# Issuing four read-back transfers from ScalarE's queue, and copying the null scores later on GpSimd

## The chip, the cores and the metric

The kernel runs on one core of one Trainium2 chip. The core has five instruction streams that run side by side and meet only at semaphores: TensorE (PE, with its weight loads shown as PEld), VectorE (DVE), ScalarE (ACT), GpSimd (POOL) and SyncE (SP). In this kernel SP does nothing but issue DMA transfers. Each stream executes in the order in which the program wrote it: an instruction that waits holds everything behind it on its own engine. The metric is device time in microseconds (us).

## The reference

64 sequences of 128 tokens and 512 features go through one attention layer with a residual:

```python
xn  = layernorm(x, g_in)
q   = (xn @ Wq).reshape(64, 128, 16, 64) * 64**-0.5     # 16 heads
k, v = split(xn @ Wkv)                                  # one head of keys and values for all
k   = concat([null_k, k]); v = concat([null_v, v])      # one null key ahead of the 128
sim = q @ k.T + concat([null_bias, attn_bias])          # (64, 16, 128, 129)
sim = where(causal or masked_key, -big, sim)            # the null key is never masked
out = softmax(sim) @ v                                  # (64, 128, 16*64)
x   = x + layernorm(out @ Wo, g_out)
```

Everything is float32.

## The kernel before, in words

**Steps and groups.** The work is a software pipeline written out by hand in `step(n)`, one step for each sequence n. Sequences are normalised and projected in groups of four, so a period is four steps, some 69 us. In one step the kernel is at several places at once: the softmax of sequence n+1, the scores of n+2, the values of n, the query projection of the group that holds n+6, and the tokens of n+11. The order of all instructions is the order of the text (`manual_schedule`); nothing is moved afterwards.

**Two matrix products in seven parts.** The query projection and the output projection are each computed as seven products of half-size blocks. Sums of blocks of the tokens (`token_sum`, xS, L403, on POOL) feed products 4 to 7. A product may be accumulated on top of an earlier one in the same PSUM tile, after the earlier one has been copied out: ACT's `keep` (L432) and `out_keep` (kyp, L725), or DVE's copy kyu (L723). So PE's seventh output product (pyX, L711) cannot start before DVE has made kyu.

**Scores.** S[b] (tile `s`, 128 partitions x 8 rows x 194 columns, two buffers) holds the scores of a sequence. POOL first writes bias plus mask into it (`bias_add`, L458, 3.45 us), then copies 16 null scores for each partition into its first and last column (`null_copy`, L467, from tile nv). DVE adds the products and takes maxima (L511, L516), ACT takes exponentials row by row (L525: eight rows of 65 for the lower half, eight of 129 for the upper), DVE inverts the sums (`rinv`, L542) and POOL scales (`scale`, L546).

**Transfers that turn things round.** The scaled weights are transposed in 32 x 32 blocks by DVE (sb, L572), and 14 transfers (`blocks_move`, L592) put the blocks in place (aTb) for PE's values (po, L641). The tokens go the same way through memory, once a group: DVE transposes 32 x 32 blocks (xb, L277), `tokens_out` (L286) writes 1 MB to a scratch tensor xd, and one step later `tokens_in` (L294) reads it back as four transfers of 256 KB into xT. `nulls_move` has ACT copy (L331, L332) and SP transfer (L333, L336) the null scores into nv.

**SP's order around the change.** In the step before: the 1 MB xd, then 14 block transfers, two stores, the residual, a sequence. In the step of the change: the four xT, two nv, and later the next 14 blocks. All of these were issued by SP.

**Semaphores of transfers.** The framework gives the transfers eight completion semaphores, handed out in the order of the program, with one transfer outstanding on each. The instruction that issues a transfer first waits until the transfer that last had its semaphore has landed, whichever engine issued that one.

Of the kernel before, what the change touches and what calls it, by code (L numbers as in the profile page):

```python
# [17 lines left out]
def kernel(  # L18
# [58 lines left out]
    nc = tc.nc  # L77
# [212 lines left out]
    def tokens_in(g):  # L290
        xT[g] = gp.tile([P, GB, KC, N], FP, tag="xT", name=f"xT_{g}")
        xd = xds.pop(g).rearrange("(i p) j e -> j p i e", p=Q)
        for j in range(NQ):
            nc.sync.dma_start(  # L294
                out=xT[g][j * Q : (j + 1) * Q].rearrange("p i c n -> p i (c n)"),
                in_=xd[j],
            )
# [27 lines left out]
    def nulls_move(g, ts):  # L325

        if ts.start == 0:
            nv[g] = hp.tile([P, GB, DH + H], FP, tag="nv", name=f"nv_{g}")
        lo, hi = slice(0, DH), slice(DH, P)
        n1, n0 = slice(DH, DH + R8), slice(DH + R8, DH + H)  # L330
        nc.scalar.copy(nv[g][lo, ts, n1], vs[g][lo, ts, n0])  # L331
        nc.scalar.copy(nv[g][hi, ts, n0], vs[g][hi, ts, n1])  # L332
        nc.sync.dma_start(  # L333
            out=nv[g][hi, ts, 0 : DH + R8], in_=vs[g][lo, ts, 0 : DH + R8]
        )
        nc.sync.dma_start(out=nv[g][lo, ts, n0], in_=vs[g][hi, ts, n0])  # L336
# [118 lines left out]
    def bias_add(b):  # L455
        g, t = divmod(b, GB)
        S[b] = sp.tile([P, R8, ROW], FP, tag="s", name=f"s_{b}")
        nc.gpsimd.tensor_tensor(  # L458
            S[b][:, :, 1 : ROW - 1],
            biasp,  # L460
            mneg[g][:, t].unsqueeze(1).broadcast_to([P, R8, NL + N]),
            ALU.add,
        )

    def null_copy(b):
        g, t = divmod(b, GB)
        nc.gpsimd.tensor_copy(  # L467
            S[b][:, :, 0 : ROW : ROW - 1],
            nv[g][:, t, DH:].rearrange("p (k e) -> p e k", k=2),
        )  # L470
# [215 lines left out]
    def out_sums(p):  # L686

        yS[p] = bp.tile([P, HC, N], FP, tag="yS", name=f"yS_{p}", bufs=1)
        h11, h12 = oT[p][:, lo_c], oT[p][:, hi_c]
        h21, h22 = oT[p + 1][:, lo_c], oT[p + 1][:, hi_c]  # L690
        nc.gpsimd.tensor_tensor(yS[p], h21, h22, ALU.add)
        nc.gpsimd.tensor_tensor(h21, h11, h21, ALU.subtract)
        nc.gpsimd.tensor_tensor(h11, yS[p], h11, ALU.subtract)  # L693
        nc.gpsimd.tensor_tensor(h12, h12, h11, ALU.subtract)

    def out_product(p, k, pool, tag, start=True):
        key = "y" + tag
        if start:
            prod[key] = pool.tile([P, HE], FP, tag=tag, name=f"py{tag}_{p}_{k}")
        a, b = oT[p], oT[p + 1] if p + 1 in oT else None  # L700
        h, w = {
            1: lambda: (a[:, lo_c], e11),
            2: lambda: (a[:, hi_c], e21),
            3: lambda: (a[:, hi_c], e22),
            4: lambda: (b[:, hi_c], wT[:, 3]),
            5: lambda: (yS[p], wT[:, 0]),
            6: lambda: (a[:, lo_c], wT[:, 1]),
            7: lambda: (b[:, lo_c], wT[:, 2]),
        }[k]()
        for c in range(HC):  # L710
            nc.tensor.matmul(  # L711
                prod[key],
                h[:, c, :],
                w[:, c, :],
                start=(start and c == 0),
                stop=(c == HC - 1),
                skip_group_check=not start,
            )
# [113 lines left out]
    def step(n):  # L832
        def ok(b, end=B):
            return 0 <= b < end
# [16 lines left out]
        if second:  # L851
            out_sums(p5673)
        elif ok(n + 2) and n >= 0:
            bias_add(n + 2)
            null_copy(n + 2)
        if third:
            pair_pow(p4)
        for m in mns:
# [37 lines left out]
        if (n + 7) % GB == 0 and 2 <= (n + 7) // GB < NG:  # L896
            tokens_in((n + 7) // GB)
# [8 lines left out]
                token_sum(qg, k)  # L906
        if second and ok(n + 2):
            bias_add(n + 2)
            null_copy(n + 2)
        if ok(n + 1) and fill:  # L910
            exps_half(n + 1, 0)
        if part == 3 and ok(n + 3):
            nulls_move((n + 3) // GB, slice(0, GB - 1))
        if part == 0 and ok(n + 2):
            nulls_move((n + 2) // GB, slice(GB - 1, GB))
        if first:
            out_product(p12, 1, ps_y, "X")
        if fast and n % 2 == 0:
# [157 lines left out]
    for n in range(-6, B - 1):  # L1076
        step(n)
        if n == -6:
            for kc in range(2):
                weights_kv(kc)  # L1080
            for kc in range(2, KC):
                weights_kv_prod(kc)
            load_late()
        if n == -5:
            for kc in range(2, KC):
                weights_kv(kc)
            causal(0)
            mask_neg(0)
            weight_sums()
# [48 lines left out]
```

## Time and profile before

| | |
|---|---|
| median of 3 runs | 1194.3 us (1191.9 to 1194.69) |
| profiled execution, its own time | 1188.5 us |
| its span | 1186.7 us |
| PE busy | 1117.3 us, 94% of the span |
| ACT busy | 684.9 us, 58% |
| POOL busy | 745.0 us, 63% |
| DVE busy | 793.4 us, 67% |
| granted TensorE clock, mean | 0.988 |
| DMA | 129.91 MB, mean 109 GB/s |

A line of a timeline reads: start, duration, engine, source line, operation, output<-inputs, shape, count, and in brackets the idle time of the engine before it and what ended that. In the tables of waits: engine, line, what it waited for, us in total, times, longest. "SPq" is SP's queue.

### The profile page before, as it was taken

The page shows a single profiled execution, that of the slowest core. Times are in us where ns is not written, and L with a number is a line of the kernel's source. Part 1 is how long each engine was busy: PE and PEld are TensorE (multiplying, and loading weights), DVE is VectorE, ACT ScalarE, POOL GpSimd, SP SyncE. Part 2 cuts the span into 40 slices and gives each one's busy share as a digit, 9 for nine tenths or more (in the row PEclk, how much of TensorE's full clock was granted, in tenths as well). Part 3 has the DMA queues.
Part 4 walks back from the last instruction along what each step waited for, and adds up shares of the span by engine and source line. Part 5 has one row for each costly group of instructions (what it writes and reads, how often), then busy time and mean ns, then how long its engine had stood idle before and what let it go on. Part 6 is the DMA issues. An engine that isn't in the chain of part 4 may idle for free.

```text
span 1186.7 us, 24481 instructions
## 1 busy us (share of the span) xinstructions
PE 1117.3 (94%) x8284; PEld 877.3 (74%) x8284; DVE 793.4 (67%) x1680; ACT 684.9 (58%) x2712; POOL 745.0 (63%) x588
## 2 busy tenths in 40 slices
PE   6877999999999999999999999999999999999786
PEld 4454787887878787887878788787878878887443
DVE  6554577676767867776776677677767756766442
ACT  3344665655666566565755656566565656655451
POOL 5454876567675756667665665767566576656432
PEclk9998999999999999999999999999999999999889
DMA  6313335343543535353353535344453533322221
GB/s 183 119 35 108 95 98 125 120 120 97 144 112 105 131 123 120 97 158 96 108 119 122 129 89 155 99 127 105 126 123 103 140 86 119 83 75 77 84 78 45
DMA packets 107852, 129.91 MB, mean 109 GB/s; under 512 B 29264, under 2 KB 72528, under 8 KB 105936
## 3 DMA queue, kind: packets, MB, share of 16 engines
q1 hardware_dynamic: 106912, 127.29, 39.2%
q8 instruction: 67, 1.10, 0.4%
q10 hardware_dynamic: 816, 1.05, 0.2%
q14 instruction: 57, 0.47, 0.1%
HBM read 54.86 MB, written 31.46 MB: 73 GB/s over the span
## 4 chain that ended last, share of the span: by engine, by line
PE 61%; SPq 12%; DMA 12%; DVE 7%; ACT 4%; POOL 2%; issue 2%; DVEq 0%; ACTq 0%; POOLq 0%
PE pa L421 13%; PE pyX L711 11%; SPq L592 10%; PE po L641 6%; PE pyY L711 6%; PE pc L421 5%; DMA xT<-xd 5%; PE ps L487 4%; PE pk L307 4%; PE py L661 3%; PE pw L421 3%; PE pyw L711 2%; DMA aTb<-sb 2%; ACT s L525 2%; PE ps L498 2%
## 5 line engine op out<-in xcount | busy, mean ns | idle before, releaser
L525 ACT ACTIVATE s<-s,nmax 128x65 f32<-128x65 f32 (+1 forms) x1024 | 372.3, 368 | 7.3 <-DVE nmax L516 6.9
L458 POOL TENSOR_TENSOR s<-biasp,mneg 128x1536 f32<-128x1536 f32 x64 | 220.9, 3451 | 127.8 <-DVE sb L572 124.9
L546 POOL TENSOR_TENSOR s<-s,rinv 128x512 f32<-128x512 f32 (+1 forms) x128 | 188.9, 1477 | 113.2 <-DVE nmro L753 81.5
L525 ACT ACTIVATION_READ_ACCUMULATOR s<-s,nmax 128x1 f32 x1024 | 194.6, 190 | 0.0
L649 ACT ACTIVATE oT<-po,nv 128x512 f32<-128x512 f32 x128 | 81.0, 680 | 166.2 <-PE po L641 166.1
L711 PE MATMUL pyX<-wT,oT 128*128 128x256 f32 x696 | 164.7, 379 | 1.2 <-POOL oT L693 0.7
L432 ACT COPY ku<-pa 128x256 f32<-128x256 f32 x120 | 44.7, 372 | 178.0 <-PE pa L421 176.4
L711 PEld LDWEIGHTS pyX<-wT,oT 128*128 128x128 f32 x696 | 131.9, 190 | 20.1 <-POOL oT L693 1.1
L511 DVE TENSOR_TENSOR s<-ps,s 128x512 f32<-128x512 f32 (+1 forms) x128 | 121.6, 950 | 26.4 <-PE ps L498 15.0
L421 PE MATMUL pa<-xS,wq 128*128 128x256 f32 x480 | 123.6, 380 | 2.4 <-ACT ku L432 1.4
L516 DVE TENSOR_REDUCE nmax<-s 128x8 f32<-128x520 f32 (+1 forms) x128 | 120.4, 940 | 6.0 <-POOL s L467 3.7
L641 PE MATMUL po<-aTb,vs 128*64 128x256 f32 (+1 forms) x768 | 109.7, 397 | 3.5 <-DMA aTb<-sb 1.8
L572 DVE STREAM_TRANSPOSE sb<-s 128x1536 f32<-128x1536 f32 x62 | 109.6, 1769 | 2.2 <-DMA xT<-xd 1.3
L421 PEld LDWEIGHTS pa<-xS,wq 128*128 128x128 f32 x480 | 86.8, 190 | 13.0 <-ACT ku L432 2.4
L487 PEld LDWEIGHTS ps<-kT,qT 64*128 64x128 f32 x1024 | 65.5, 196 | 31.6 <-issue 20.7
L487 PE MATMUL ps<-kT,qT 64*128 64x128 f32 x1024 | 78.1, 294 | 5.4 <-DVE s L511 5.4
L442 DVE TENSOR_TENSOR qT<-pw,kp 128x256 f32<-128x256 f32 x60 | 25.4, 423 | 77.2 <-ACT kp L432 77.2
L641 PEld LDWEIGHTS po<-aTb,vs 128*64 128x64 f32 (+1 forms) x768 | 44.9, 138 | 39.5 <-issue 27.3
L421 PE MATMUL pc<-xS,wS 128*128 128x256 f32 x240 | 63.3, 386 | 7.8 <-POOL xS L403 6.9
L245 POOL TENSOR_TENSOR rstd<-rstd,nhalf 128x1 f32<-128x1 f32 x64 | 35.8, 559 | 54.7 <-DVE rstd L244 54.7
L307 PE MATMUL pk<-wkv,xT 128*128 128x144 f32 x488 | 69.9, 286 | 0.0
L421 PE MATMUL pa<-xS,wS 128*128 128x256 f32 x240 | 67.8, 405 | 0.0
(122 smaller groups left out, 2162.5 us busy)
## 6 DMA issues: line engine op xcount, KB each, us to landing
aTb<-sb SPq DMA_DIRECT2D x372, 64.0 KB
x<-in_x_dram SPq DMA_DIRECT2D x64, 256.0 KB
res<-in_x_dram SPq DMA_DIRECT2D x64, 256.0 KB
out_dram<-y SPq DMA_DIRECT2D x64, 256.0 KB
aTb<-sb SPq DMA_DIRECT2D x496, 32.0 KB
xd<-xb SPq DMA_DIRECT2D x14, 1024.0 KB
xT<-xd SPq DMA_DIRECT2D x56, 256.0 KB
wo<-in_L_cond_Wo_dram SPq DMA_DIRECT2D x1, 2048.0 KB
```

What stands on the lines that cost most here:

```text
L307: nc.tensor.matmul(pkv, xT[g][:, t, kc, :], wkv[:, kc, :], start=(kc == 0), stop=(kc == KC - 1),)
L421: nc.tensor.matmul(prod[tag], w[:, kc, f * P : (f + 1) * P], t[:, :, kc, :], start=(start and kc == 0), stop=(kc == HK - 1), skip_group_ch ...
L458: nc.gpsimd.tensor_tensor(S[b][:, :, 1 : ROW - 1], biasp, mneg[g][:, t].unsqueeze(1).broadcast_to([P, R8, NL + N]), ALU.add,)
L487: nc.tensor.matmul(pv[:, r, f, :], qT[g][rows, f, t, 1].rearrange("p u i -> p (u i)"), kT[b][rows, :], start=True, stop=True,)
L511: nc.vector.tensor_tensor(sv, pss.pop((b, hf)), sv, ALU.add)
L516: nc.vector.tensor_reduce(nmax[b][:, hf], S[b][:, :, WITH_NULL[hf]], AX.X, ALU.max, negate=True)
L525: nc.scalar.activation(row, row, AF.Exp, bias=nmax[b][:, hf, k : k + 1], accum_out=rsum[b][:, hf, k : k + 1],)
L546: nc.gpsimd.tensor_tensor(sv, sv, rinvs.pop((b, hf)).unsqueeze(2).broadcast_to([P, R8, sv.shape[2]]), ALU.mult,)
L572: nc.vector.transpose(sb.rearrange("p j e q -> p e j q"), S[b][:, :, 1 : ROW - 1].rearrange("p e (j k) -> p e j k", k=Q),)
L592: nc.sync.dma_start(out=aT_of(b)[dst, is_].rearrange("p s e q -> p s (e q)"), in_=sb[src, js].rearrange("p s e q -> p s (e q)"),)
L641: nc.tensor.matmul(po[u][r * DH : (r + 1) * DH, half], vals, aT_of(b)[rows, slots, r * NF : (r + 1) * NF], start=True, stop=True,)
L711: nc.tensor.matmul(prod[key], h[:, c, :], w[:, c, :], start=(start and c == 0), stop=(c == HC - 1), skip_group_check=not start,)
```

## The change

Two edits. `tokens_in` issues its four transfers from ACT's queue in place of SP's, at the same place of the text; on ACT this is between two runs of four lower exponentials of sequence n+1. And `null_copy(n + 2)` is written later in the step, behind POOL's lower scaling, the first two token sums and the calls of `nulls_move`. No operation is added or left out.

```diff
@@ tokens_in
         for j in range(NQ):
-            nc.sync.dma_start(
+            nc.scalar.dma_start(
                 out=xT[g][j * Q : (j + 1) * Q].rearrange("p i c n -> p i (c n)"),
                 in_=xd[j],
             )
@@ step
         elif ok(n + 2) and n >= 0:
             bias_add(n + 2)
-            null_copy(n + 2)
...
         if second and ok(n + 2):
             bias_add(n + 2)
-            null_copy(n + 2)
         if ok(n + 1) and fill:
             exps_half(n + 1, 0)
         if part == 3 and ok(n + 3):
             nulls_move((n + 3) // GB, slice(0, GB - 1))
         if part == 0 and ok(n + 2):
             nulls_move((n + 2) // GB, slice(GB - 1, GB))
+        if ok(n + 2) and n >= 0:
+            null_copy(n + 2)
```

In the built program of the changed kernel, the four issues on ACT have these waits, in every group from the second read-back on: the first for xd and for the first of the 14 block transfers of the step before; the second for the seventh of them; the third for the eleventh; the fourth for the fourteenth. In the first read-back the last of the block transfers is waited for by the fourth issue too.

## The prediction

> **What bounds the kernel now.** I read the page's busy line first, then the chain that ended last, then the waits of PE, POOL and SP, and at last one group of four steps on the timeline.
>
> ```profile
> PE 1117.3 (94%) x8284; PEld 877.3 (74%) x8284; DVE 793.4 (67%) x1680; ACT 684.9 (58%) x2712; POOL 745.0 (63%) x588
> PE 61%; SPq 12%; DMA 12%; DVE 7%; ACT 4%; POOL 2%; issue 2%; DVEq 0%; ACTq 0%; POOLq 0%
> ```
>
> PE bounds it. From 150 to 1030 us, the steady part, PE is busy for 863.9 of 880 us. So about 16 us there, some 18 for all 14 groups that read tokens back, are the most that shorter waits can give; a delay that PE sees costs its full length.
>
> ```profile
> PE po L641 <- DMA aTb<-sb: 18.3, 11, 5.1
> PE pc L421 <- POOL xS L403: 6.9, 9, 1.9
> POOL s L467 <- DMA nv<-vs: 51.5, 12, 5.4
> SPq L592 <- DMA xT<-xd: 22.9, 42, 1.3
> ```
>
> These are what the change aims at. SP's block issues (L592) end waits on the read-back 42 times, three in each of 14 groups. That is the semaphore rule at work: an issue is held until the landing of the transfer that last used its semaphore. In the group at 523 us the four xT, by the trace's landing events, land at 531.3, 532.3, 533.7 and 534.5, and SP issues its 3rd to 6th block at 531.28, 532.34, 533.72 and 534.48. So the blocks are late, and with them PE's po; POOL's null copy waits for nv, queued behind the same read-back, and holds the token sums that PE's pc needs.
>
> **The change, first part: the read-back on ACT.** Taken away from SP: four issues, 1.9 us in a group, in front of two nv transfers and 14 blocks. Put on ACT, after the qT copy:
>
> ```profile
> 515.52 0.37 ACT L439 COPY qT<-pa 128x256 f32<-128x256 f32 x1
> 515.79 0.35 ACT L525 ACTIVATE s<-s,nmax 128x65 f32<-128x65 f32 x1
> ...
> 518.35 0.35 ACT L725 COPY kyp<-pyY 128x256 f32<-128x256 f32 x1
> ...
> 519.38 0.36 ACT L432 COPY kp<-pa 128x256 f32<-128x256 f32 x1
> ...
> 526.78 1.27 ACT L649 ACTIVATE oT<-po,nv 128x512 f32<-128x512 f32 x2 [4.33 <-PE po L641]
> ```
>
> ACT reaches the place at 515.8. But the fourth issue waits for the fourteenth block of the step before, and SP is then in the middle of issuing those:
>
> ```profile
> 512.04 9.04 SPq L592 DMA_DIRECT2D aTb<-sb  x14
> 521.13 1.08 SPq L791 DMA_DIRECT2D out_dram<-y  x2
> 522.25 0.45 SPq L125 DMA_DIRECT2D res<-in_x_dram  x1
> 522.75 0.60 SPq L119 DMA_DIRECT2D x<-in_x_dram  x1
> 523.45 1.88 SPq L294 DMA_DIRECT2D xT<-xd  x4
> ```
>
> By the landing events the first block lands at 514.1, the 7th at 517.8, the 11th at 520.4 and the 14th at 522.6; xd landed at 513.8. So the first issue passes at once, and the fourth is held until 522.6. Over the 13 groups that follow the first, that landing is 6.7 to 7.6 us, in the mean 7.0, behind ACT's arrival. One issue takes 0.43 to 0.5 us with 0.1 around it, so ACT resumes 7.0 + 0.6 = 7.6 us late.
>
> Behind it on ACT stand twelve exponentials, two null copies, kyp and kp. DVE waits for kp, and PE for DVE:
>
> ```profile
> 519.77 0.42 DVE L442 TENSOR_TENSOR qT<-pw,kp 128x256 f32<-128x256 f32 x1 [1.91 <-ACT kp L432]
> 520.82 0.42 DVE L723 COPY kyu<-pyX 128x256 f32<-128x256 f32 x1 [0.62 <-PE pyX L711]
> 521.48 1.89 PE L711 MATMUL pyX<-wT,oT 128*128 128x256 f32 x8
> ```
>
> DVE makes qT as soon as kp is there, then kyu, and PE's seventh output product starts 0.24 us after kyu. The one reserve on this path is the 0.62 us that DVE waited for PE. So PE stands still for 7.6 - 0.6 = 7.0 us in each group. The exponentials end, the upper scaling runs and sb is made as much later, so nothing catches up; ACT's 4.33 us of idle time ahead of oT comes too late on this path.
>
> Two costs are added for which no row stands. Blocks and read-back now share the DMA engines. Between 516 and 520 us the engines are 0.27 busy, so I take 0.4 us more for the 14th landing; nothing at one end, 2 us at the other (the 2.0 us that one transfer's issue to landing takes, once more). And an idle PE loses its clock:
>
> ```profile
> 562.70 0.38 PE L641 MATMUL po<-aTb,vs 64*64 64x256 f32 x2
> 563.02 1.08 PE L641 MATMUL po<-aTb,vs 128*64 128x256 f32 x8
> 564.04 1.16 PE L487 MATMUL ps<-kT,qT 64*128 64x128 f32 x16
> ...
> 1143.01 1.12 PE L641 MATMUL po<-aTb,nv 64*64 64x256 f32 x4 [4.53 <-DVE y L773]
> 1144.05 1.97 PE L641 MATMUL po<-aTb,vs 128*64 128x256 f32 x8
> 1145.96 2.08 PE L487 MATMUL ps<-kT,qT 64*128 64x128 f32 x16
> ```
>
> After 4.53 us of idle time the same work, 0.65, 1.08 and 1.16 us when the clock is up (0.65 is the same row at 1122 us), takes 0.5 + 0.9 + 0.9 = 2.3 us more; after 5.14 us (at 93 us) 1.8 and after 3.61 (at 1127) 2.0. Two gaps of 2.3 and 2.65 us cost nothing. At 7 us I take 2.0, between 0 and 2.3.
>
> The sum: 13 x (7.0 + 0.4 + 2.0) = 122 us. In the first group (ACT arrives at 109.7, the 14th block lands at 115.5) PE already waits 2.65 us for blocks, so I take 4 there, 2 to 7.
>
> What it gives: xT lands some 7 us earlier and the next 14 blocks start after it, so SP's waits and PE's po waits go (6.4 us of them in the steady part, and 2 for the clock lost at 543). The store, which takes over a semaphore from the first xT, finds it landed.
>
> On splitting queues the Trainium skill (DMA: Bandwidth & Descriptors, Issuing engines are not separate DMA queues) says that transfers from all engines run on the same 16 DMA engines and that a second issuing engine saves only the time to issue. That speaks against a gain beyond SP's 1.9 us a group, 27 us at most; the rows put the gain elsewhere, in landings that hold SP's issues, and the loss in a wait on ACT that the rule doesn't mention. By the rule alone the sum would lie between 1162 and 1189 us on the profiled execution.
>
> **Second part: the null copy.** It moves on POOL past two small powers, the lower scaling and, once a group, two token sums; no transfer and no other queue is passed. The copy takes 0.2 us. Its reader is DVE's lower maximum, some 10 us later in the step, so lateness up to 5 us is covered. The sums no longer stand behind a wait for nv: PE's pc waits go, 4.1 us in the steady part. In steps with no wait nothing changes.
>
> Gains together: at least 4 us (pc alone), at most 18 to 20 (all of PE's idle time and the clock loss). I take 13, the two named waits with the clock loss.
>
> Sum: 1188.5 + 122 + 4 - 13 = 1301 us for the profiled execution. That execution was 5.8 us below the median, so 1307 us against 1194.3.
>
> **The rivals.**
> 1. *Only the issues cost.* The blocks would have to land before ACT's arrival. Then ACT loses 4 x 0.5 = 2.0 us, PE 1.4, in 14 groups 20 us, against 13 of gain: 1201. For it: the first three issues do find their landings within 4.6 us, while ACT has slack later. Against it: the fourteenth block is issued at 520.5, 4.7 us after ACT's arrival.
> 2. *The change pays.* If ACT's delay stays under DVE's 0.62 us, PE loses nothing and the waits go: 1194 - 18 = 1176. It decides where the delay falls below about 1.5 us a group (0.6 of reserve, 0.9 of gain). For it: 51.5 and 22.9 us of waits on POOL and SP do go. Against it: four issues alone take 2.0 us.
> 3. *The stall is smaller than I count.* PE keeps its clock, or the engines use the pause to work off what made PE wait elsewhere: 1188.5 + 13 x 7.0 + 2 - 20 + 5.8 = 1267 at the least.
> 4. *It spreads.* Contention takes its 2 us in all groups: 1188.5 + 13 x 11.3 + 7 - 4 + 5.8 = 1344.
>
> **How the numbers follow.** My forecast, 1285 to 1330, has 0.60; rival 3 (1250 to 1285) 0.17; rival 4 0.11; rival 1 0.06; rival 2 0.06. The range that leaves out no more than 0.2 goes from 1255 to 1335. A measurement of this kernel can tell 0.3%, 3.6 us, from no change. Slower gets the forecast, 3, 4 and half of rival 1: 0.91; faster rival 2: 0.06; the same 0.03.
>
> **What the profile after would show.** Right: in each group ACT idle for about 7 us ahead of L525 with a block transfer as releaser; DVE's qT waiting for kp about as long; PE idle for about 7 us ahead of pyX with kyu (L723) as releaser, 14 times, 90 to 105 us together; matmuls after it at nearly double time and the mean clock below 0.988; SP's waits on xT, POOL's on nv and PE's on xS near nothing. Wrong: if ACT's idle time is about 2 us a group, the issues aren't held and rival 1 holds; if ACT is held and PE isn't, there is a reserve that I missed; if PE stalls and its clock stays, the sum is some 26 us too high.

## The result, and the profile after

The changed kernel takes 1323.0 us (median of 4 runs, 1320.8 to 1323.93), the kernel before in the same comparison 1194.5 us. The ratio is 1.1098, with a 95% interval from 1.1053 to 1.1144: 11% slower. The profiled execution took 1322.9 us, its span is 1320.8 us, and the mean granted clock is 0.937 (0.988 before).

The page of the changed kernel: its span, the busy line, the granted clock by slices, the shares of the chain that ended last, and the costliest group of instructions (after the bars: busy us and mean ns of one, then the idle time ahead of it with what ended that).

```profile
span 1320.8 us, 24479 instructions
PE 1144.6 (87%) x8284; PEld 897.9 (68%) x8284; DVE 789.9 (60%) x1680; ACT 686.0 (52%) x2712; POOL 744.4 (56%) x588
PEclk9988989989899898989989898998989989899979
PE 67%; SPq 10%; DMA 7%; ACT 7%; DVE 5%; issue 2%; POOL 1%; ACTq 0%; DVEq 0%; POOLq 0%
...
L711 PE MATMUL pyX<-wT,oT 128*128 128x256 f32 x696 | 189.3, 420 | 121.1 <-DVE kyu L723 120.4
```

Every engine does the work it did before, with the same count of instructions. PE is busy 27.3 us longer for the same 8284 matmuls: the clock, which stands at 8 tenths or less in 16 of the 40 slices (3 before). The queue of ACT, where the transfers now are, has 0% of the chain; so the share of a queue does not show this loss.

The waits of PE, ACT and DVE in the changed kernel (what for, us in total, times, longest):

```profile
PE pyX L711 <- DVE kyu L723: 120.4, 14, 10.0
PE po L641 <- DMA aTb<-sb: 9.5, 4, 5.1
...
PE po L641 <- DMA nv<-vs: 7.1, 1, 7.1
...
ACT s L525 <- DMA out_dram<-y: 124.1, 12, 11.0
...
DVE rinv L542 <- ACT s L525: 164.9, 64, 10.6
DVE qT L442 <- ACT kp L432: 82.6, 57, 2.8
```

The growth of the span, 134.1 us, is made of three parts. PE waits 120.4 us for kyu ahead of pyX, where before it waited 0.5. Thirteen of the fourteen gaps are new; they measure 7.67 to 10.03 us, in the mean 9.22, and make 119.9 us. PE's busy time gives 27.3 us, of which 24.6 lie in the group that follows the gap (189.3 against 164.7 us). The rest, 13.1 us less, is net of the first group, where PE now waits 7.1 us (by the line for nv) and waited 2.65 for a block: PE's other waits are 17.5 us shorter. The group in the kernel before:

```profile
L711 PE MATMUL pyX<-wT,oT 128*128 128x256 f32 x696 | 164.7, 379 | 1.2 <-POOL oT L693 0.7
```

One group of the changed kernel on the timelines of SP, ACT, DVE and PE (start, duration, and in brackets the idle time before and what ended it; "ACTq" is ACT's queue):

```profile
570.08 9.05 SPq L592 DMA_DIRECT2D aTb<-sb  x14
```

```profile
573.51 0.37 ACT L439 COPY qT<-pa 128x256 f32<-128x256 f32 x1
573.57 10.46 ACTq L294 DMA_DIRECT2D xT<-xd  x4
584.08 0.35 ACT L525 ACTIVATE s<-s,nmax 128x65 f32<-128x65 f32 x1 [10.20 <-DMA out_dram<-y]
```

```profile
585.55 0.20 DVE L542 RECIPROCAL rinv<-rsum 128x8 f32<-128x8 f32 x1 [9.74 <-ACT s L525]
...
588.06 0.42 DVE L442 TENSOR_TENSOR qT<-pw,kp 128x256 f32<-128x256 f32 x1 [2.31 <-ACT kp L432]
588.40 0.42 DVE L723 COPY kyu<-pyX 128x256 f32<-128x256 f32 x1
```

```profile
576.92 1.89 PE L711 MATMUL pyX<-wT,oT 128*128 128x256 f32 x8
578.65 1.03 PE L421 MATMUL pc<-xS,wS 128*128 128x256 f32 x4
588.88 3.78 PE L711 MATMUL pyX<-wT,oT 128*128 128x256 f32 x8 [9.20 <-DVE kyu L723]
592.45 2.34 PE L711 MATMUL pyY<-wo,oT 128*128 128x256 f32 x8
```

Read from top to bottom: SP is still issuing its 14 block transfers when ACT reaches the read-back at 573.57. ACT's four issues take until 584.03 and then the exponentials go on. DVE stands at rinv, then at qT, then makes kyu; PE starts 9.20 us late, and its first eight matmuls take 3.78 us in place of 1.89, the next eight 2.34: 2.3 us for the clock.

What ended ACT's wait is the point at which the line misleads. It names the store, because a store's event was the last seen just then. In the program the fourth issue of this group waits for the fourteenth block of the step before; the trace has that block landing at 583.70 and the fourth issue at 583.73. SP had issued this block at 578.51, so it was 5.19 us on its way. In the group at 523 us of the kernel before, it was issued at 520.47 and landed at 522.55: 2.08 us. In the mean of the 13 later groups it is 5.0 us against 2.1. The 3.1 us between them are in no row of the kernel before.

The text ahead of the prediction is wrong for two of the 14 read-backs. In the first, the fourth issue waits for the eleventh block, the third for the first transfer of the read-back itself, and none for the fourteenth block. In the last, the fourth issue (at 1131.82) waits for the read-back's own second transfer (landed at 1131.80), and the fourteenth block lands only at 1133.57; ACT is idle for 8.7 us there and PE for 7.67. In the other 12 the fourth issue follows the landing of the fourteenth block.

### The profile page after: what moved, and what is told of

It reads as the page before. It is cut to its first block, busy times and chain, and to the rows that moved or that the text cites. A ratio compares the mean times of both kernels' runs of the same rounds, so it can differ in the third digit from the quotient of the medians.

```text
span 1320.8 us, 24479 instructions
## 1 busy us (share of the span) xinstructions
PE 1144.6 (87%) x8284; PEld 897.9 (68%) x8284; DVE 789.9 (60%) x1680; ACT 686.0 (52%) x2712; POOL 744.4 (56%) x588
## 3 DMA queue, kind: packets, MB, share of 16 engines
q8 instruction: 66, 1.08, 0.4%
## 4 chain that ended last, share of the span: by engine, by line
PE 67%; SPq 10%; DMA 7%; ACT 7%; DVE 5%; issue 2%; POOL 1%; ACTq 0%; DVEq 0%; POOLq 0%
PE pyX L711 15%; PE pa L421 13%; SPq L592 10%; PE pyY L711 6%; PE po L641 6%; PE pc L421 5%; ACT s L525 5%; PE ps L487 4%; DMA aTb<-sb 4%; PE pk L307 3%; PE pyw L711 3%; PE pw L421 3%; PE py L661 3%; PE ps L498 2%; DVE sb L572 2%
## 5 line engine op out<-in xcount | busy, mean ns | idle before, releaser
L711 PE MATMUL pyX<-wT,oT 128*128 128x256 f32 x696 | 189.3, 420 | 121.1 <-DVE kyu L723 120.4
L711 PEld LDWEIGHTS pyX<-wT,oT 128*128 128x128 f32 x696 | 144.8, 211 | 149.7 <-DVE kyu L723 126.0
L542 DVE RECIPROCAL rinv<-rsum 128x8 f32<-128x8 f32 x128 | 24.0, 189 | 165.0 <-ACT s L525 164.9
```

What stands on the lines that cost most here:

```text
L711: nc.tensor.matmul(prod[key], h[:, c, :], w[:, c, :], start=(start and c == 0), stop=(c == HC - 1), skip_group_check=not start,)
```

## The experiments

All of them compute the whole reference. Where one run of a kernel stands, it is its profiled execution; the kernel before had medians of 1192.1 to 1196.5 us beside them.

**1. Each edit alone.** Before, with only the queue changed:

```diff
-            nc.sync.dma_start(
+            nc.scalar.dma_start(
```

> Only the first edit: the four read-back issues on ACT, the null copy at its old place. Theory (ACT held by the semaphores of the block transfers): the whole loss is here, PE's idle time ahead of pyX with kyu as releaser again about 120 us in 14 gaps, 1323 us within 4, since nv now lands well before POOL comes to the null copy. Rival (the late null copy has a share in the loss): clearly below 1315 us.

It took 1323.8 us. The waits of PE in this kernel:

```profile
PE pyX L711 <- DVE kyu L723: 119.3, 14, 10.2
...
PE po L641 <- DVE qT L442: 7.4, 1, 7.4
```

Before, with only the null copy moved:

```diff
         elif ok(n + 2) and n >= 0:
             bias_add(n + 2)
-            null_copy(n + 2)
...
+        if ok(n + 2) and n >= 0:
+            null_copy(n + 2)
```

> Only the second edit: the null copy late, the read-back on SP as before. Theory: PE's waits on the token sums (pc <- xS, 6.9 us) shrink to the 1.9 us of the start, PE's waits on aTb stay near 18 us, the time falls by 2 to 6 us to about 1190. Rival (the late copy holds DVE's lower maxima): above 1198, with DVE waits on POOL L467 of more than 10 us.

It took 1196.7 us (12 runs), a ratio of 1.0009 (0.9968 to 1.005). The waits of PE in this kernel:

```profile
PE po L641 <- DMA aTb<-sb: 21.1, 11, 5.1
...
PE pc L421 <- POOL xS L403: 2.6, 2, 1.9
```

The whole loss is in the first edit. The second does what it says: POOL's waits for nv are gone and PE's pc waits fall from 6.9 to 2.6 us. But the 2 to 6 us that I expected from it do not show in the time; PE's waits for blocks were 18.3 us and are 21.1 in this one profile.

**2. The hold without the bytes.** The read-back stays on SP (on top of the null copy alone), and ACT gets something else to wait for at the place where the changed kernel has its four issues. The first try gave it four unused transfers of 512 bytes:

```diff
...
+            for k in range(4):
+                nc.scalar.dma_start(out=tiny[:, k], in_=cond[0:2])
```

> The read-back is on SP as before, the null copy late; at the place on ACT stand four transfers of 512 bytes, which wait for the 8th, 10th, 12th and 14th block transfer of the step before. No bytes to speak of are added. Theory: ACT is held until the 14th block has landed, undisturbed: its idle time there about 7.4 us, PE's gap ahead of pyX 6.9 us in the mean, the clock loss on top, about 1296 us, 1283 to 1306. What is missing from 1323 is then the delay that the read-back's own bytes put on the blocks (PE's gap was 9.2). Rival (the transfers' bytes hold the engines): no gaps, 1190 to 1205 us.

It took 1199.1 us. Waits of PE and ACT in this kernel (lines are one further down):

```profile
PE pyX L712 <- DVE kyu L724: 22.0, 14, 3.2
...
ACT s L526 <- DMA tiny<-in_cond_dram: 26.7, 11, 3.1
```

The expectation had the waits wrong. With four more transfers in the program, the semaphores fall differently: these issues wait for the 1st, 3rd, 5th and 7th block, and ACT is held only until the seventh lands. The miss is the experiment's, not the theory's: it gives a small dose, in the group at 525 us and most others 2.19 us of hold and 1.23 us of gap on PE.

The second try holds ACT with a copy of one 32 x 1 column out of the last block, and adds no transfer:

```diff
...
+            nc.scalar.copy(held, aT_of(n)[3 * Q :, 1, 0, 0:1])
```

> The read-back is on SP as before, the null copy late; at the place on ACT stands one copy of 32x1 that reads what the 14th block transfer of the step before wrote, so that ACT waits for its landing and for nothing else, and no transfer is added. Theory: ACT idle for about 6.8 us there in 14 places (the 14th landing was 7.0 us behind ACT's arrival in the trace of before), PE's gap ahead of pyX about 6.3 us, the clock loss on top: 1300 us, 1285 to 1312. What then is missing from PE's gap of 9.2 us is the delay that the read-back's bytes put on the 14th block (it landed 5.2 us after its issue there, 2.1 before). Rival (the transfers on ACT's queue themselves, not the hold, make most of the loss): below 1240 us.

It took 1284.5 us, just below what was expected. Waits of PE and ACT in this kernel:

```profile
PE pyX L712 <- DVE kyu L724: 80.0, 14, 7.0
PE po L642 <- DMA aTb<-sb: 9.6, 4, 5.1
...
ACT held L898 <- DMA aTb<-sb: 94.9, 14, 7.8
```

Without any read-back on ACT, a wait for the fourteenth block alone makes 80.0 of the 120.4 us. The other 40 us come with the read-back on ACT's queue: here ACT is held for 6.8 us in the mean, there for 10.2. Three doses stand side by side:

| kernel | ACT held, us | PE's gap, us |
|---|---|---|
| four small transfers (7th block), typical group | 2.2 | 1.2 |
| one copy (14th block) | 6.8 | 6.1 |
| the change (in 12 groups the 14th block, behind the read-back) | 10.2 | 9.2 |

PE's gap is 0.7 to 1.0 us shorter than the hold. The forecast had it 0.6 us shorter (ACT 7.6 us late with the issue, PE 7.0).

**3. The path from ACT to PE.** The changed kernel, with kyu ahead of the qT that waits for kp on DVE:

```diff
             keep("a", "p1")
-            q_out(qg, f, lo_t, "w", "p1")
+            if not second:
+                q_out(qg, f, lo_t, "w", "p1")
...
             out_keep("X", "yu2", "yu2")
+            if fast:
+                q_out(qg, f, lo_t, "w", "p1")
```

> The changed kernel, but in every second step DVE makes kyu ahead of the qT that waits for ACT's kp. ACT's hold stays at 10.2 us. Theory (PE pays through kp, qT, kyu): kyu now waits only for the inversion behind ACT's lower exponentials, some 2.8 us earlier, PE's gap ahead of pyX falls from 9.2 to about 6.4 us, the time to about 1284 us, 1275 to 1295. Rival (PE waits for something else that ACT's hold delays): the gap stays within 1 us of 9.2 and the time above 1312 us.

It took 1291.7 us. Waits of PE and ACT, and DVE's timeline, in this kernel:

```profile
PE pyX L711 <- DVE kyu L723: 82.8, 14, 6.7
...
ACT s L525 <- DMA out_dram<-y: 122.7, 12, 10.4
```

```profile
573.47 0.20 DVE L542 RECIPROCAL rinv<-rsum 128x8 f32<-128x8 f32 x1 [9.91 <-ACT s L525]
573.59 0.37 DVE L723 COPY kyu<-pyX 128x256 f32<-128x256 f32 x1
575.97 0.42 DVE L442 TENSOR_TENSOR qT<-pw,kp 128x256 f32<-128x256 f32 x1 [2.01 <-ACT kp L432]
```

ACT is held as long as in the changed kernel, and PE's gap falls from 9.2 to 6.4 us: the step from kp over qT to kyu carried 2.8 us of it. What is left comes over DVE's rinv, which stands ahead of kyu and waits for the four lower exponentials that ACT does behind the issues. So the path in the prediction was the last to end, and a second one ends 2.8 us earlier.

**4. The same four issues, later on ACT.** The changed kernel, with the call of `tokens_in` behind the step's normalisation, where the blocks have long been issued:

```diff
-        if (n + 7) % GB == 0 and 2 <= (n + 7) // GB < NG:
-            tokens_in((n + 7) // GB)
...
         for m in mns:
             norm_apply(m)
+        if (n + 7) % GB == 0 and 2 <= (n + 7) // GB < NG:
+            tokens_in((n + 7) // GB)
```

> Both edits, but the four read-back issues stand on ACT behind the normalisation of the tokens, where ACT sat idle for 4.3 us. By their semaphores they now wait for the 11th and the 14th block, a store and the second nv transfer. Theory: the first three pass within 1 us of ACT's arrival; the fourth is held until nv has landed, about 7 us, so that oT comes 3 us late and PE waits some 2 us a group ahead of its key projection, without the clock loss: about 1215 us, 1195 to 1240; no gaps ahead of pyX. Rival (any four transfers on ACT cost what these did): above 1290 us.

It took 1275.8 us. Waits of PE, and ACT's timeline, in this kernel:

```profile
PE pk L341 <- ACT oT L649: 69.4, 14, 6.9
```

```profile
565.21 12.59 ACTq L294 DMA_DIRECT2D xT<-xd  x4
577.84 1.27 ACT L649 ACTIVATE oT<-po,nv 128x512 f32<-128x512 f32 x2 [11.88 <-DMA aTb<-sb]
```

The gaps ahead of pyX are gone, and new ones stand ahead of pk, behind ACT's oT. At this place the fourth issue waits for the second nv transfer. SP issued it at 567.63, behind a residual and a sequence on its own queue and the read-back's first three transfers on ACT's, and it landed at 577.47, 9.8 us later. The expectation had about 7 for the hold, which was 11.9. In the kernel before, the transfer issued at 543.22, behind a residual, a sequence and a mask but with no read-back, took 4.4 us; so the read-back seems to delay the small transfer for which the last of its own issues waits, though its bytes were not tried apart at this place. Moving the issues changes which wait is paid. The clock (0.952) was not in the expectation either.

**5. One issue in place of four.** Both edits, with the scratch tensor laid out so that SP writes it in four transfers and ACT reads it back in one of 1 MB, at the same place. This issue waits for xd and for an old load, and for no block:

```diff
...
-        for j in range(NQ):
-            nc.scalar.dma_start(
-                out=xT[g][j * Q : (j + 1) * Q].rearrange("p i c n -> p i (c n)"),
-                in_=xd[j],
-            )
+        nc.scalar.dma_start(
+            out=xT[g].rearrange("p i c n -> p i (c n)"), in_=xds.pop(g)
+        )
```

> Both edits, but the scratch tensor has another layout: SP writes it with four transfers of 256 KB and ACT reads it back with one of 1 MB, from the same place. This one issue waits for xd and an old load, and for no block transfer. Same bytes on the same queue. Theory: ACT's idle time at this place falls from 10.2 us to under 1, PE's gaps ahead of pyX go, the gains stay: about 1181 us, 1172 to 1190. Rival (1 MB on ACT's queue beside the blocks is what costs, through slower landings): PE gaps ahead of po of 3 us or more a group, above 1230 us.

It took 1189.9 us (12 runs), a ratio of 0.9981 (0.9954 to 1.0007). The 11% are gone, and with them every gap ahead of pyX: the loss was in the issue's wait, not in the engine that issues. But what should now be gained is not measurable. Waits of PE, DVE and SP, and DVE's timeline, in this kernel:

```profile
PE ps L487 <- DVE s L511: 18.6, 15, 3.1
...
DVE y L734 <- DMA out_dram<-y: 102.9, 28, 6.5
...
SPq L592 <- DMA xT<-xd: 33.6, 13, 3.8
```

```profile
530.88 0.42 DVE L734 TENSOR_TENSOR y<-pyX,kyp 128x256 f32<-128x256 f32 x1 [6.51 <-DMA out_dram<-y]
```

The same wait of DVE in the kernel before:

```profile
DVE y L734 <- DMA out_dram<-y: 65.2, 24, 5.5
```

DVE writes the output into y, which has three buffers, and waits until the store that last used the buffer has landed. In this kernel ACT issues the 1 MB at 518.16, and it lands at 523.70. Four blocks that SP issues between 518.48 and 520.37 land at 523.89 to 524.40, all of them after it. SP's next issue, at 523.72, comes before any of these four has landed; it takes over the semaphore of the 1 MB and waits for that landing. SP is held so in 13 groups, 33.6 us in all. So its stores go out late, and by the trace DVE's y is late, then DVE's s, and PE waits 18.6 us ahead of ps (5.4 before). The semaphore rule that held ACT in the changed kernel here holds SP. The same with the call of `tokens_in` moved behind the normalisation, as in 4:

> One read-back issue as in the kernel with the other scratch layout, but behind the normalisation of the tokens, 6.7 us later on ACT. Its semaphores are those of xd and of the fifth block, all landed by then. Theory for the lost gain of that kernel (the 1 MB runs ahead of the last blocks, holds SP's issues and with them the stores, for which DVE's y waits, 103 us there and 65 before): here the blocks and the stores are issued ahead of the 1 MB, DVE's waits for stores fall to 65 us or less, PE's waits ps <- DVE s go from 18.6 to under 8 us, the time is 1180, 1172 to 1190. Rival (the gain isn't to be had, PE is simply full): within 0.3% of before.

It took 1193.8 us (12 runs), 0.9985 (0.9955 to 1.0015). DVE's wait in this kernel:

```profile
DVE y L734 <- DMA out_dram<-y: 92.0, 27, 7.0
```

DVE's waits were expected to fall to those of the kernel before; they didn't. The stores are delayed from the later place too, now on their way: the second of the two, issued at 524.12, 0.1 us ahead of the 1 MB, took 5.3 us to land, and at 521.81 in the kernel before 2.45.

**6. The new wait taken away.** A fourth buffer for y (and one less of six for kT, to make room), with the one issue at its two places, and in the kernel before as a control:

```diff
-        kT[m] = hp.tile([P, N], FP, tag="kT", name=f"kT_{m}", bufs=6)
+        kT[m] = hp.tile([P, N], FP, tag="kT", name=f"kT_{m}", bufs=5)
...
-            ys[b] = hp.tile([P, DIM], FP, tag="y", name=f"y_{b}", bufs=3)
+            ys[b] = hp.tile([P, DIM], FP, tag="y", name=f"y_{b}", bufs=4)
...
```

> The kernel with one read-back issue on ACT (both edits, other scratch layout), and a fourth buffer for the output tile y, so that DVE's y needs the landing of an older store; one of six kT buffers goes for the room. Theory (the gain of that kernel was lost to the stores, which the 1 MB delays: DVE y <- out_dram 103 us, PE ps <- DVE s 18.6 us in 15 places): DVE's waits for stores fall below 30 us, PE's ps <- DVE s to about 5, and the time to about 1180, 1172 to 1188. Rival (what PE gains in one place it waits in another, or the gain is below the noise): within 0.4% of before.

> The kernel before with the fourth y buffer and five kT buffers, nothing else: the control. Theory: DVE's waits for stores fall from 65 to below 30 us, but PE waits for DVE s only 5.4 us before, so the time stays within 0.4% of before. Rival (the y buffer alone is worth what the other kernel gains): faster than before by over 0.5%.

> The kernel with one read-back issue behind the normalisation of the tokens, and the fourth y buffer. Theory: DVE's waits for stores fall from 92 to below 30 us, PE's ps <- DVE s from 14.3 to about 5, the time to about 1184, 1176 to 1191. Rival: within 0.4% of before.

| kernel | median, us | ratio to before, 95% |
|---|---|---|
| one issue, 4 buffers | 1167.1 (6 runs) | 0.9757 (0.9725 to 0.979) |
| before, 4 buffers | 1191.7 (12 runs) | 0.9944 (0.9913 to 0.9976) |
| one issue later, 4 buffers | 1170.5 (6 runs) | 0.9786 (0.9746 to 0.9825) |

Waits of PE and DVE with one issue and 4 buffers:

```profile
PE ps L487 <- DVE s L511: 3.6, 1, 3.6
...
DVE y L734 <- PE pyX L711: 48.6, 28, 2.0
```

Waits of PE in the kernel before with 4 buffers:

```profile
PE po L641 <- DMA aTb<-sb: 16.5, 8, 5.1
...
PE pc L421 <- POOL xS L403: 7.6, 10, 1.9
```

In the first, DVE's y waits for PE and no longer for a store; in the second, the waits for blocks and sums stay as they were. One issue alone gives 0.2%, which can't be told from nothing; a fourth buffer alone 0.6%, more than the 0.4% allowed for in its expectation; both together 2.4%, more than expected (1180): each hides what the other frees. The two versions with both are the fastest of all, and can't be told apart. They also have the late null copy and the other layout; what these add to the 2.4% was not tried apart.

Busy time in the steady part, from 150 to 1030 us, of the kernel before, of the changed one and of one issue with 4 buffers (the window and its length; then PE, PEld, DVE, ACT and POOL, each with its count; granted clock, DMA share, GB/s):

```profile
150.00:1030.00 880.00, 863.94 (x6609) 705.13 (x6606) 630.44 (x1346) 545.20 (x2170) 580.98 (x458) 1.00 0.43 117
```

```profile
150.00:1030.00 880.00, 777.03 (x5801) 633.30 (x5801) 550.41 (x1185) 477.78 (x1899) 514.95 (x405) 0.94 0.36 103
```

```profile
150.00:1030.00 880.00, 879.54 (x6799) 722.94 (x6798) 646.85 (x1368) 555.40 (x2214) 600.33 (x471) 1.00 0.41 119
```

In the last, PE is busy for all but 0.5 of 880 us. The stretch holds 2.9% more matmuls than in the kernel before, but not the same ones. Counted through, the 6607 matmuls that start in it in the kernel before take 880.1 us there, 864.1 of them busy, and 857.3 us in the last kernel, 856.9 busy. So 22.8 us are gained, 15.6 of them waits and 7.2 inside what the profile counts as busy, and the "about 16 us" of the prediction was no upper bound for this part. What it is within the busy time was not tried. Over the whole profiled executions PE's busy time is the same (1117.3 and 1118.4 us), so some 8 us more are spent outside the steady part; the two spans are 15.4 us apart, the medians 29.

## Why the prediction was right, point by point

**The hold.** Right in place and cause: in 12 of the 14 groups the fourth issue waits for the fourteenth block, and experiment 2 gives most of the loss by that wait alone. ACT stands idle for 10.2 us, where the working had 7.0 for the landing, 0.4 for contention and 0.6 for the issue, which took 0.31.

**The contention.** This is the term that was mis-sized: 0.4 us, at most 2. The fourteenth block comes 3.1 us later than before. The working took the mean load of the DMA engines from a kernel in which no read-back runs at that time. In the changed kernel ACT's second read-back transfer is issued at 577.72 and lands at 581.87, the third is issued at 578.48 and lands at 583.45; the fourteenth block, issued at 578.51, lands 0.25 us after that. By these landings the wait for the block is in good part one for ACT's own transfers. PE's gap is 9.22 us where the sum had 7.0 + 0.4: 13 x 1.82 = 24 us more. The landing alone would have made some 2.6 us a group; the shorter issue and the larger reserve on the path took 0.7 off.

**The path to PE.** Right, by experiment 3. PE's gap is 1.0 us shorter than ACT's idle time, where the working had 0.6; without this the miss would be 5 us larger. Some of it shows in the lines: PE starts 0.06 us after kyu, and in the kernel before 0.24 us after it. That a second path ends 2.8 us earlier was not in the working.

**The clock.** 26 us forecast (13 x 2.0), 27.3 measured, net of the clock losses elsewhere. The Trainium skill (TensorE: Matmul & The Clock Gate, What's actually happening) has the clock halved after an idle window of about 3.4 us; the gaps of 9.2 us here agree, with 3.78 us for work of 1.89.

**The first group.** 4 us forecast, 4.4 measured (7.1 - 2.65). It stands ahead of po, not ahead of pyX. The line that names nv misleads: by the landing events nv had not landed when PE started at 121.35, and DVE's qT, which waits for kp, had ended 0.06 us before. With the queue alone changed the same wait is put down to qT (7.4 us). So here too PE pays for ACT's hold, 5.3 us in this group.

**The gain.** 13 us forecast between 4 and 20, 17.5 measured. Whether it came for the reason given can't be told in this kernel. PE's waits for blocks fall from 18.3 to 9.5 us. They fall to 9.6 us also in the kernel of experiment 2 that leaves the read-back on SP and holds ACT: a pause of PE, in which the engines ahead of it can catch up, is enough. But in the steady part they also all but go (0.2 us, 6.4 before) with the one issue and the four buffers of experiment 6, where PE has no such pause: so the pause is not needed. The pc waits fall to 2.9 us with the first edit alone and to 2.6 with the second alone, and the second alone gave no measurable time.

**Together.** The forecast's sum of 1301 for the profiled execution, with 24 us more for the gaps, 1.3 for the clock, 0.4 for the first group and 4.5 us more of gain, is 1322; the profiled execution has 1322.9.

**The rivals.** Rival 4 had the steady part right: 11.3 us a group, against 9.22 + 27.3 / 13 = 11.3 measured. Its time, 1344, was too high because it had a gain of 4 us and 7 for the first group, and because it added 5.8 us for a profiled execution below the median: the profiled execution of the changed kernel is at its median. Rival 3's sum of "1267 at the least" does not fit its range, which begins at 1250. That the result lies in the forecast's own span, 1285 to 1330, is in part luck: contention was taken too low, and a gain above the forecast made up for 4.5 us of it. With the gain of 13 it would be 1327, with that of 4 some 1336, outside the stated range. Rival 1 (only the issues cost) and rival 2 (the change pays) fall with ACT's 10.2 us. But rival 2's point, a delay under 1.5 us a group, is met by the one issue of experiment 5 (0.33 us), and even there nothing measurable is gained until the stores are dealt with: the gain that it named had a further cover, DVE's wait for stores, which neither the rivals nor the forecast had.

## What to carry to other kernels

Before a transfer is moved to a compute engine's queue, look up which transfers its issue waits for, when the last of those lands, and what stands behind the issue on that engine: here one wait for a transfer that another queue was just issuing cost 9.2 us of PE and 2 us of clock in each group. If a read-back has to stand there, make it one transfer that waits for nothing recent, and look up too which later issue takes over its semaphore: here that held SP for 2.6 us a group. When a wait is removed and the time stays the same, look for the buffer that is now last to come free; here one more output buffer turned a gain too small to measure into 2.4%.

## What the runs showed of the hardware that was not expected

- Small transfers issued on one queue just after a large one on another landed only when the large one had. In the group at 518 us of experiment 5, blocks issued 0.3 to 2.2 us after the 1 MB read-back landed 0.2 to 0.7 us after it, 4.0 to 5.4 us after their issue, where a block took about 2 us before. The Trainium skill (DMA: Bandwidth & Descriptors, Queues, rings and completion order) has the engines take turns between queues packet by packet; these landings don't look like a fair share by bytes. How the packets were cut was not tried.
- The issue of the same transfer (L294) takes 0.31 us on ACT and 0.43 us on SP, in the median. That is the only gain of the other queue that the trace shows directly: 0.5 us a group.
- A gap of 1.42 us at 543 us in the kernel before cost PE its clock (1.79 us for work of 1.08), while gaps of 2.3 and 2.65 us did not. So the length of a gap alone does not say whether the clock is lost. After the gaps of 5.8 to 10 us ahead of pyX in the changed kernel and in experiments 2 and 3 the next sixteen matmuls always took longer, by 1.4 to 3.1 us.
